# Value's evacuation and its planes in the attention stage: half strips side by side, the last 32 channels moved by DMA

## The chip, the cores and the metric

The kernel runs on one core of a Trainium2 chip. Its time is the device time of one execution in microseconds (us). A core has a tensor engine (PE, with its weight loads listed as PEld), a vector engine (DVE), a scalar engine (ACT), GpSimd (POOL), and the queue engine SP, which issues most of the DMAs. Each engine works through its own instructions in order and waits for others through semaphores. PE writes to PSUM; DVE and ACT read it, POOL does not.

## The reference

Input x is 4 images of 96 channels by 128 x 128 pixels. Layer 0 adds a selective state-space block (scans in four directions over 192 inner channels) to x. Layer 1 adds an attention convolution, and the change lies in that layer:

```python
xr, x1, x2 = _relu_split_norm(x, sc1, sc2, res_coef, nc1, nc2)
# in _attn_conv(x1, x2, aw1, aw2, aw3), every _conv2d being 3x3 over 96 channels:
key = _unfold_nonoverlap(_conv2d(x1, aw1, pad), K).reshape(B, C, kk, -1)
qry = _unfold_nonoverlap(_conv2d(x2, aw2, pad), K).reshape(B, C, kk, -1)
attn = jnp.einsum('bckl,bqkl->bqck', key, qry)
attn = jax.nn.softmax(attn.reshape(B, C, C * kk) / sqrt(C * kk), axis=2)
value = _conv2d(x1, aw3, pad)
y1 = conv2d(value, attn as 3x3 weights)          # per image
y2 = layer_norm(_conv2d(x2, w_conv2, K // 2)) * x1
out = xr + _conv2d(concat(layer_norm(y1), y2), w_full, 0) + b_full
```

So four convolutions are made from the two maps x1 and x2: key and value from x1, query and the second convolution ("c2") from x2. Value is then convolved once more, with weights that depend on all of key and query.

## The kernel before

**Stages.** First come projections and scans of layer 0, then image 0's convolutions by nine taps (direct_maps), and from about 3670 us the attention of the images: image 0's last convolution, and for images 1 to 3 a map stage and a last convolution each. While one image is in attention ("left"), the next image's output projection, its norm and split (ssm_output, split_norm) and the previous image's final output run beside it ("light"). co_run interleaves the two streams by costs that the generators yield; the order in which instructions are written, and a scheduler that puts each engine's instructions in a fixed order before the run, set what every engine does next.

**Convolution by planes.** A row of 128 pixels is cut in TW = 4 runs of TN = 32 with a border element each (pitch PB = 33, row PP = 132). From it planes_of builds NP = 6 sums, the planes, of 32 elements per row: ACT scales the tile into x4 and x2 (scaled, L1404 and L1405), POOL forms ten sums and differences (differences and sums, L1413 to L1418 and L1383), and store_planes writes them to DRAM (L1426 on SP). x4, x2 and pl are single tiles where value is concerned (bufs=1). A later convolution loads planes (ya, yc), and six small products per position replace nine taps. products writes them to three PSUM tiles "two", of which the pool has three buffers; outputs then copies the tiles "ends" and "odd" to SBUF on ACT (L1526) and combines them on DVE into four interleaved outputs (L1540 to L1548, four scalar_tensor_tensor per output part).

**The map stage.** A strip is AR = 12 rows (the eleventh has 8), handled in the order map 0 (x1), map 1 (x2). For each map, "first" products give 128 output channels of the whole strip: 96 of key or query and, in partitions 96 to 128, the last 32 of value or c2. They go to a ring tile of two strips, whose rows are stored by remainder of three (row pitch JW = 135, runs at pitch JB = 34), and PairTaps later transposes and multiplies them into the attention logits sm. The "second" products give the first 64 channels of value or c2 for both half strips at once, in partitions 0 to 64 and 64 to 128. Later is a queue of callbacks: each tick of products runs what is due, `later(f, n)` runs f n ticks after the next one.

**Value and c2 before.** All of value is gathered in own, 128 x 12 rows x 132: the last 32 channels by four POOL copies per strip from the ring to own[96:128] (L1983, after cut has zeroed a border at L1725), the first 64 by the evacuation of the second products to own[0:64], one part per half strip:

```python
to = [(64 * q, 64 * q + 64, vv[0:64, q * hr : (q + 1) * hr]) for q in range(2)]
```

value_out then builds planes of each half strip over all 128 partitions, the second three ticks after the first, and stores them in two DMAs each (vp<-pl). c2's last 32 channels use partitions 64 to 96 of own: four POOL copies (L1983) and one DMA (L1987) per strip; its first 64 go to oc as 128 x 192.

**Constants.** zeros is 133 wide and clears the borders of the DRAM maps with one DMA each (new_map L1262, where L388 to L391); mean192 is 96 wide.

Of the kernel before, what the change touches and what calls it, by code (L numbers as in the profile page):

```python
# [9 lines left out]
F32 = mybir.dt.float32  # L10
# [7 lines left out]
C = 96  # L18
# [53 lines left out]
def kernel(  # L72
# [87 lines left out]
    mean192 = filled(1.0 / (2 * C), "mean192")  # L160
    zeros = filled(0.0, "zeros", PW + 4)
# [6 lines left out]
    signs = const.tile([128, 1], F32, name="signs", tag="signs")  # L168
    nc.vector.memset(signs[64:96], 1.0)
    nc.vector.memset(signs[96:128], -1.0)  # L170
    eps = const.tile([128, 1], F32, name="eps", tag="eps")
    nc.vector.memset(eps, LN_EPS)

# [48 lines left out]
    def other_weights():  # L222
# [9 lines left out]
        with (  # L232
            tc.tile_pool(name="w0", bufs=1, side="right") as w0,
            tc.tile_pool(name="ps0", bufs=1, space=PSUM, side="right") as ps0,
        ):
            wf = w0.tile([RANK, NK, 2 * C], F32, name="wf")
            nc.gpsimd.dma_start(wf, dt_wT)
            outw = w0.tile([C, 2, C], F32, name="outw")
            nc.sync.dma_start(outw, out_wT)
            one = w0.tile([3, 128], BF16, name="one")  # L240
            nc.vector.memset(one, 1.0)
            nc.vector.memset(wdt, 0.0)
            nc.vector.memset(wbc, 0.0)
            yield
            flat = "p k c -> p (k c)"
            pieces = split3(w0, wf.rearrange(flat), [RANK, NK * 2 * C])
            for row, ch, g, p, n in (
                (row, *part)
                for img, *part in PARTS
                for row in ((KI * img,) if part[1] == 1 else (0, 64))  # L250
            ):
                for w in range(3):
                    yield
                    src = pieces[w].rearrange("p (k c) -> p k c", k=NK)[:, :, ch : ch + n]
                    for i in range(3):
# [14 lines left out]
            nc.vector.tensor_add(outbs, pb, outb)  # L270

            pw = ps0.tile([C, C], F32, name="pw")
            for j in range(2):
                nc.tensor.matmul(
                    pw, lhsT=mean192, rhs=outws[:, j], start=(j == 0), stop=(j == 1)
                )
            nc.vector.tensor_sub(outws, outws, pw.unsqueeze(1).to_broadcast([C, 2, C]))
        yield wdt, wbc, outws, outbs
# [75 lines left out]
    def project_weights(pool):  # L354
# [4 lines left out]
        with tc.tile_pool(name="wq", bufs=1, side="left") as pq:  # L359
# [28 lines left out]
            nc.sync.dma_start(where[:, 0:PW], zeros[0:1, 0:PW])  # L388
# [3 lines left out]
            nc.sync.dma_start(where[:, (H + 1) * PW :], zeros[0:1])  # L392
# [869 lines left out]
    def new_map(name):  # L1262

        m = dram.tile([C, (H + 2) * PW + 4], F32, name=name, tag=name, bufs=1)
        nc.sync.dma_start(m[:, 0:PW], zeros[:, 0:PW])
        nc.sync.dma_start(m[:, (H + 1) * PW :], zeros[:, 0 : PW + 4])
        return m

    def new_planes(name):
# [92 lines left out]
                eng.dma_start(w3[p : p + 32, j], wd[64:96, 2, i])  # L1362
        return w1, w2, w3

    def planes_of(later, pool, t, r, then, most=RS, vector=False, bufs=2, p=C):

        a2 = AA * AA
        v = t[:, : r * PP].rearrange("p (h x) -> p h x", x=PP)  # L1370

        def planes(name, bufs):
            pl = pool.tile([p, NP, most * TN], F32, name=name, bufs=bufs)[:, :, : r * TN]
            return pl, [pl[:, i].rearrange("p (h t) -> p h t", t=TN) for i in range(NP)]

        def sums(eng, mid, outer, to):
            f1, f2 = mid[:, :, 0:TN], mid[:, :, PB : PB + TN]
            f3, f0 = outer[:, :, 0:TN], outer[:, :, TN:]
# [20 lines left out]
            later(lambda: then(pl))  # L1399

        def scaled():
            x4 = pool.tile([p, most * PP], F32, name="x4", bufs=bufs)[:, : r * PP]
            x2 = pool.tile([p, most, 2, PB], F32, name="x2", bufs=1)[:, :r]
            nc.scalar.mul(x4, t[:, : r * PP], a2)  # L1404
            nc.scalar.mul(x2, v.rearrange("p h (k b) -> p h k b", b=PB)[:, :, 0:TW:2], AA)  # L1405
            later(lambda: differences(x4.rearrange("p (h x) -> p h x", x=PP), x2))

        def differences(x4, x2):
            mid, outer = x4[:, :, : 2 * PB], x4[:, :, 2 * PB : 2 * PB + 2 * TN]
# [3 lines left out]
            sub(mid, v[:, :, 2 * PB :], mid)  # L1413
            sub(outer, v[:, :, 1 : 1 + 2 * TN], outer)
            sub(to[4], v[:, :, 3 * PB : 3 * PB + TN], v[:, :, PB : PB + TN])
            sub(d1, x2[:, :, 1, 0:TN], d1)
            add(to[3], to[4], d1)
            sub(to[4], to[4], d1)  # L1418
# [278 lines left out]
    class PairTaps(Taps):  # L1697
# [3 lines left out]
        def __init__(self, ps, later, pool):  # L1701
            self.ps, self.later, self.pool = ps, later, pool
            self.taps = [(0, 5), (5, KK)]
            self.sm = pool.tile([C, KK, C], F32, name="sm")
            self.rings = [
                pool.tile([128, 2, AR, JW], F32, name=f"ring{i}", tag=f"ring{i}") for i in range(2)
            ]
# [225 lines left out]
    def attention(img, at):  # L1933
# [4 lines left out]
        def both(*fs):  # L1938
            return lambda: [f() for f in fs if f]

        own = p1.tile([128, AR * PP], F32, name="own")
        if not img.mapped:
            taps = PairTaps(ps, later, pm)
            nc.gpsimd.memset(own, 0.0)
            last = own[64:96, : AR * W]
            vv = own.rearrange("p (h j b) -> p h j b", j=TW, b=PB)[:, :, :, 0:TN]

            def value_out(r0, r):

                def f():  # L1950
                    hr = r // 2
                    for i, a in enumerate((0, hr)):

                        def then(pl, a=a):
                            store_planes(nc.sync, img.vp[0:64], r0 + a, hr, pl[0:64])
                            store_planes(nc.sync, img.vp[64:96], r0 + a, hr, pl[96:128])

                        later(planes_of(
                            later, pm, own[:, a * PP :], hr, then, AR // 2, bufs=1, p=128
                        ), 3 * i)  # L1960

                return f

            for s, (r0, r) in enumerate(chunks):
                hr = r // 2
                for m in (0, 1):
# [2 lines left out]
                    to = taps.rows(m, s, r3)  # L1969

                    def first_out(m=m, s=s, r0=r0, r=r, r3=r3, to=to):
                        if m:
                            for j, v in enumerate(to):
                                nc.vector.bn_stats(
                                    img.c2a[96:128, TW * (r0 // AR) + j], v[96:128, :r]
                                )
                            d = last.rearrange("p (h j t) -> p h j t", j=TW, t=TN)
                        else:
                            taps.cut(s, r3)
                            d = vv[96:128]  # L1980
                        d = d[:, :r3].rearrange("p (i q) j t -> p q i j t", q=3)
                        for j, v in enumerate(to):
                            nc.gpsimd.tensor_copy(  # L1983
                                d[:, :, :, j], v[96:128].rearrange("p (q i) t -> p q i t", q=3)
                            )
                        if m:
                            nc.sync.dma_start(  # L1987
                                img.c2d[64:96, r0 * W : (r0 + r) * W], last[:, : r * W]
                            )

                    evac = outputs(
                        p2, 128, r3 * TN, [(0, 128, to)], later, first_out
# [647 lines left out]
```

## Time and profile before

| what | value |
|---|---|
| median of 3 runs | 6518.25 us (6508.8 to 6521.92) |
| the profiled execution | 6520.08 us, of which its span is 6518.3 us |
| granted clock of PE, mean over the span | 0.886 |
| value's plane builds on ACT, L1404 with L1405 | 66 of each, 863 and 543 ns |
| value and c2 copies on POOL, L1983 | 264, 505 ns |
| value's evacuation of second products, L1548 | 64x192, mean 351 ns (3840 to 4150 us) |
| store of c2's last 32 channels, L1987 | 33 issues on SP, 0.318 us each |

Times are given from the start of the span. In a row of groups, a name such as `own<-ring` is the tile written and the tile read, then come shapes as partitions x elements, the count, the busy time and the mean of one. In a timeline row, the first two numbers are start and duration, and the bracket at its end is the time the engine sat idle before it and what released it. In a source view, "sat idle before it until" lists who released the line's instructions, the idle time in us and how often.

### The profile page before, as it was taken

To read this page: it belongs to the slowest core of one execution; us is meant where nothing else is said; L and a number is where in the kernel's file an instruction comes from. 1 tells how busy PE (TensorE), PEld (TensorE's weight loads), DVE (VectorE), ACT (ScalarE), POOL (GpSimd) and SP (SyncE) were. 2 spreads that over 40 slices of the span, in tenths; PEclk is the share of its full clock that TensorE was granted. 3 is DMA by queue.
4 is the path that set the end of the run, shared out by engine and by line. 5 is a ranking of instruction groups with operands and counts; after the bars stand their busy time and mean duration, and the time that the engine had idled before them with its cause. 6 is when DMAs were issued, how large, how long until landed. Compare 5 with 4: busy or idle time off the path is not lost. (4 is left out here: it accounts for less than half of the span.)

```text
span 6518.3 us, 76253 instructions
## 1 busy us (share of the span) xinstructions
PE 5323.7 (82%) x23264; PEld 2300.7 (35%) x23264; DVE 4813.2 (74%) x7265; ACT 3816.2 (59%) x4800; POOL 3426.6 (53%) x2799
## 2 busy tenths in 40 slices
PE   6889988987887845989988588877878777888888
PEld 2333323322222111444433234444333444344553
DVE  4247778988998768989745885587774787887766
ACT  1247768777787676777624564476544664544642
POOL 2236757978888546969621444456133474033320
PEclk9999989998998666999998788988988888999989
DMA  7766777775766757675666766655776555865658
GB/s 160 175 158 185 199 206 195 217 205 162 219 179 170 218 162 225 197 208 173 200 190 184 195 193 164 171 154 159 198 203 168 151 153 157 223 179 147 185 151 217
DMA packets 865060, 1198.52 MB, mean 184 GB/s; under 512 B 215598, under 2 KB 716054, under 8 KB 852172
## 3 DMA queue, kind: packets, MB, share of 16 engines
q1 hardware_dynamic: 841036, 1138.70, 63.8%
q0 software_dynamic: 16208, 38.42, 2.2%
q10 hardware_dynamic: 7408, 16.53, 0.8%
q8 instruction: 187, 3.06, 0.2%
q14 instruction: 221, 1.81, 0.1%
HBM read 777.82 MB, written 345.62 MB: 172 GB/s over the span
## 5 line engine op out<-in xcount | busy, mean ns | idle before, releaser
L624 PE MATMUL bank<-y,wp 128*128 128x512 f32 (+3 forms) x3584 | 1312.4, 623 | 85.6 <-DMA y<-y 34.9
L857 POOL TENSOR_TENSOR y<-y,dl 128x1024 f32<-128x1024 f32 x384 | 1057.1, 2753 | 267.3 <-DVE dl L849 244.1
L824 POOL TENSOR_TENSOR dl<-dl,u 128x1024 f32<-128x1024 f32 x384 | 1010.4, 2631 | 252.8 <-ACT dA L800 124.1
L845 DVE TENSOR_TENSOR_SCAN dA<-dA,pBC 128x512 f32<-128x512 f32 x768 | 981.6, 1278 | 30.7
L1453 PE MATMUL two<-ya,wd 128*64 128x192 f32 (+3 forms) x2376 | 591.2, 425 | 222.5 <-ACT odd L1526 116.5
L624 PEld LDWEIGHTS bank<-y,wp 128*128 128x128 f32 (+3 forms) x3584 | 457.3, 169 | 753.0 <-issue 651.8
L738 PE MATMUL pBC<-xr,wbc 60*128 60x512 bf16 (+1 forms) x1536 | 462.2, 405 | 315.6 <-DVE dA L845 243.3
L849 DVE TENSOR_TENSOR dl<-dA,pBC 128x512 f32<-128x512 f32 x768 | 528.4, 688 | 258.2 <-PE pBC L738 185.8
L2112 PE MATMUL bank<-y,wn 128*64 128x384 f32 (+5 forms) x2408 | 673.8, 505 | 53.2 <-DMA y<-x1d 28.1
L1912 ACT COPY yb<-ya 64x768 f32<-64x768 f32 (+1 forms) x660 | 537.8, 815 | 207.5 <-PE two L1453 123.0
L667 ACT ACTIVATE dl<-pd,dtb 128x512 f32<-128x512 f32 x768 | 486.2, 684 | 188.7 <-PE pd L738 172.8
L1453 PE MATMUL two<-yb,wd 128*64 128x192 f32 (+3 forms) x2376 | 562.4, 407 | 1.9 <-ACT yb L1912 1.9
L828 DVE TENSOR_TENSOR pBC<-dl,pBC 128x512 f32<-128x512 f32 x768 | 527.6, 687 | 7.3 <-POOL dl L824 6.3
L2112 PEld LDWEIGHTS bank<-y,wn 128*64 128x64 f32 (+3 forms) x2408 | 309.3, 168 | 345.5 <-issue 178.5
L800 ACT ACTIVATE dA<-dl,negA 128x1024 f32<-128x1024 f32 x384 | 420.3, 1141 | 2.3
L1453 PEld LDWEIGHTS two<-ya,wd 128*64 128x64 f32 (+1 forms) x2376 | 265.2, 171 | 433.4 <-ACT odd L1526 126.1
L738 PEld LDWEIGHTS <-wbc 60*128 60x128 bf16 (+1 forms) x1536 | 103.6, 96 | 762.7 <-issue 749.5
L667 ACT ACT_TABLE_LOAD x248 | 318.2, 1283 | 92.1 <-PE pd L738 78.1
L2221 POOL MEMSET o<- 1x1024 f32 x60 | 56.4, 947 | 573.6 <-PE bank L2276 244.5
L1453 PEld LDWEIGHTS two<-yb,wd 128*64 128x64 f32 (+1 forms) x2376 | 293.0, 171 | 146.2 <-issue 34.4
L1004 PE MATMUL bank<-y,outws 96*96 96x512 f32 x512 | 307.7, 737 | 8.2 <-DVE r L1017 6.0
L1383 POOL TENSOR_TENSOR pl<-x 128x192 f32<-128x192 f32 (+2 forms) x456 | 307.8, 690 | 0.2
(317 smaller groups left out, 9532.9 us busy)
## 6 DMA issues: line engine op xcount, KB each, us to landing
u<-zb SPq DMA_DIRECT2D x192, 1024.0 KB
yms<-y SPq DMA_DIRECT2D x96, 512.0 KB
y<-yms SPq DMA_DIRECT2D x64, 768.0 KB
xn<-xnew SPq DMA_DIRECT2D x128, 384.0 KB
ya<-vp SPq DMA_DIRECT2D x120, 336.0 KB
y<-y SPq DMA_DIRECT2D x128, 258.2 KB
zb<-z SPq DMA_DIRECT2D x64, 512.0 KB
ya<-x1p SPq DMA_DIRECT2D x90, 336.0 KB
```

Source lines behind the costliest of these rows:

```text
L624: nc.tensor.matmul(blocks(pz[p:e]), lhsT=ws[k][:, d, c : c + e - p], rhs=window(ys[k], at, d, n), start=(i == 0), stop=(i == len(terms) - 1),)
L667: nc.scalar.activation(dst, src, AF.Softplus, bias=bias)
L738: nc.tensor.matmul(p, lhsT=w[rows], rhs=xr[rows, at : at + CH], start=True, stop=True)
L800: nc.scalar.activation(live[m]["dA"], live[m]["dl"], AF.Exp, scale=negA[:, g % 3, k : k + 1])
L824: nc.gpsimd.tensor_mul(t, t, u_view(n))
L828: nc.vector.tensor_mul(p, live[n]["dl"][:, bass.ts(half, CH)], p)
L845: nc.vector.tensor_tensor_scan(h, h, p, init, ALU.mult, ALU.add)
L849: nc.vector.tensor_mul(live[n]["dl"][:, sl], live[n]["dA"][:, sl], live[n]["C", half])
L857: nc.gpsimd.tensor_add(v, v, t.rearrange("p (a b) -> p a b", b=W))
L1453: nc.tensor.matmul(of(to[p:e], r), lhsT=w[:, i, c : c + e - p], rhs=tiles(t[k][PAIR[i]][:, SLOT[i]], o, r), start=(k == 0), stop=False,)
L1912: nc.scalar.copy(yb[k][64 * h - 64 : 64 * h, :, :n], ya[k][0:64, :, h * TN : h * TN + n])
L2112: nc.tensor.matmul(pc[p:e, :n].rearrange("p (h w) -> p h w", w=W), lhsT=w[:, c : c + e - p], rhs=v[:, :, 0:W], start=(i == 0), stop=(i == ...
```

## The change

Value's first 64 channels are evacuated as one part of 128 partitions: the first half strip in partitions 0 to 64, the second in 64 to 128 of a tile of six rows. One plane build serves both. The last 32 channels are not copied by POOL; DMAs on SP move the ring's rows, with the ring's pitch, into a second tile, few, in which four half strips (those of two strips) stand in partitions 0, 32, 64 and 96. After every second strip, and after the last, one build makes the planes of all of them, three ticks after the other build. planes_of takes the pitch as arguments for this. c2's last 32 channels use partitions 96 to 128 of the tile sm, which were unused: for each third of the ring's rows one POOL copy to one of two slots there, and one DMA from it. The evacuation of the first products, the order of products and all costs that pace co_run stay. To make room, zeros is 72 wide and maps are cleared in two DMAs each, mean192 is 32 wide with a full one made where it is needed, and signs, which nothing reads, is gone.

```diff
+    def clear(to):
+        for a in range(0, to.shape[1], 72):
+            v = to[:, a : min(a + 72, to.shape[1])]
+            nc.sync.dma_start(v, zeros[: v.shape[0], : v.shape[1]])
...
-    def planes_of(later, pool, t, r, then, most=RS, vector=False, bufs=2, p=C):
+    def planes_of(later, pool, t, r, then, most=RS, vector=False, bufs=2, p=C, pb=PB, pp=PP):
...
-            self.sm = pool.tile([C, KK, C], F32, name="sm")
+            sm = pool.tile([128, KK, C], F32, name="sm")
+            self.sm = sm[0:C]
+            self.spare = sm[96:128].rearrange("p t o -> p (t o)")
...
-        own = p1.tile([128, AR * PP], F32, name="own")
+        half = AR // 2
+        own = p1.tile([128, half * (PP + JW)], F32, name="own")
...
-                    for i, a in enumerate((0, hr)):
-                        def then(pl, a=a):
-                            store_planes(nc.sync, img.vp[0:64], r0 + a, hr, pl[0:64])
-                            store_planes(nc.sync, img.vp[64:96], r0 + a, hr, pl[96:128])
-                        later(planes_of(
-                            later, pm, own[:, a * PP :], hr, then, AR // 2, bufs=1, p=128
-                        ), 3 * i)
+                    later(planes_of(
+                        later, pm, first, hr, stores(0, 64, halves), half, bufs=1, p=128
+                    ))
+                    to = [(r0 - r, hr), (r0 - hr, hr)] + halves if s % 2 else halves
+                    if s % 2 or r0 + r == H:
+                        n = 32 * len(to)
+                        later(planes_of(
+                            later, pm, few[:n], hr, stores(64, 96, to), half, bufs=1, p=n,
+                            pb=JB, pp=JW,
+                        ), 3)
...
+            def value_rows(s, r, v):
+                def f():
+                    hr, slots = r // 2, (r + 2) // 3
+                    for i in range(slots):
+                        for h in range(2):
+                            a, e = max(3 * i, h * hr), min(3 * i + 3, (h + 1) * hr)
+                            if a < e:
+                                k = 32 * (2 * (s % 2) + h)
+                                nc.sync.dma_start(
+                                    few[k : k + 32, (a - h * hr) * JW : (e - h * hr) * JW],
+                                    v[:, i + (a - 3 * i) * slots : i + (e - 1 - 3 * i) * slots + 1 : slots],
+                                )
+                return f
+
+            def c2_rows(r0, r, v):
+                slots = (r + 2) // 3
+                for i in range(slots):
+                    n = min(3, r - 3 * i)
+                    t = taps.spare[:, i % 2 * 3 * W : (i % 2 * 3 + 3) * W]
+                    nc.gpsimd.tensor_copy(
+                        t.rearrange("p (q j t) -> p q j t", j=TW, t=TN),
+                        blocks(v[:, i], 3, slots * JW, JB, TW, TN),
+                    )
+                    at = (r0 + 3 * i) * W
+                    nc.sync.dma_start(img.c2d[64:96, at : at + n * W], t[:, : n * W])
...
-                            d = last.rearrange("p (h j t) -> p h j t", j=TW, t=TN)
+                            c2_rows(r0, r, v)
                         else:
                             taps.cut(s, r3)
-                            d = vv[96:128]
-                        for j, v in enumerate(to):
-                            nc.gpsimd.tensor_copy(
-                                d[:, :, :, j], v[96:128].rearrange("p (q i) t -> p q i t", q=3)
-                            )
-                        if m:
-                            nc.sync.dma_start(
-                                img.c2d[64:96, r0 * W : (r0 + r) * W], last[:, : r * W]
-                            )
+                            later(value_rows(s, r, v), 1)
...
-                        to = [
-                            (64 * q, 64 * q + 64, vv[0:64, q * hr : (q + 1) * hr])
-                            for q in range(2)
-                        ]
-                        then = value_out(r0, r)
+                        to = [(0, 128, vv[:, :hr])]
+                        then = value_out(s, r0, r)
```

More of the change, by code (lines that the diff above doesn't have):

```diff
@@ L159 @@
     mean96 = filled(1.0 / C, "mean96")
-    mean192 = filled(1.0 / (2 * C), "mean192")
-    zeros = filled(0.0, "zeros", PW + 4)
+    mean192 = filled(1.0 / (2 * C), "mean192", 32)
+    zeros = filled(0.0, "zeros", 72)
+    def clear(to):
+        for a in range(0, to.shape[1], 72):
+            v = to[:, a : min(a + 72, to.shape[1])]
+            nc.sync.dma_start(v, zeros[: v.shape[0], : v.shape[1]])
     patches = const.tile([128, 1], F32, name="patches", tag="patches")
@@ L166 @@
         nc.sync.dma_start(patches[p : p + 1], zeros[0:1, 0:1])
-    signs = const.tile([128, 1], F32, name="signs", tag="signs")
-    nc.vector.memset(signs[64:96], 1.0)
-    nc.vector.memset(signs[96:128], -1.0)
     eps = const.tile([128, 1], F32, name="eps", tag="eps")
@@ L270, in other_weights @@
             nc.vector.tensor_add(outbs, pb, outb)
+            mean = w0.tile([C, C], F32, name="mean")
+            nc.vector.memset(mean, 1.0 / (2 * C))
             pw = ps0.tile([C, C], F32, name="pw")
@@ L274, in other_weights @@
                 nc.tensor.matmul(
-                    pw, lhsT=mean192, rhs=outws[:, j], start=(j == 0), stop=(j == 1)
+                    pw, lhsT=mean, rhs=outws[:, j], start=(j == 0), stop=(j == 1)
                 )
@@ L387, in project_weights @@
             where = dram.tile([1, (H + 2) * PW + 4], F32, name="where", bufs=1)
-            nc.sync.dma_start(where[:, 0:PW], zeros[0:1, 0:PW])
+            clear(where[:, 0:PW])
             nc.sync.dma_start(
@@ L391, in project_weights @@
             )
-            nc.sync.dma_start(where[:, (H + 1) * PW :], zeros[0:1])
+            clear(where[:, (H + 1) * PW :])
             taps = dram.tile([KK + 1, H * PW], F32, name="taps", bufs=1)
@@ L1264, in new_map @@
         m = dram.tile([C, (H + 2) * PW + 4], F32, name=name, tag=name, bufs=1)
-        nc.sync.dma_start(m[:, 0:PW], zeros[:, 0:PW])
-        nc.sync.dma_start(m[:, (H + 1) * PW :], zeros[:, 0 : PW + 4])
+        clear(m[:, 0:PW])
+        clear(m[:, (H + 1) * PW :])
         return m
@@ L1363, in product_stack, with blocks @@
         return w1, w2, w3
-    def planes_of(later, pool, t, r, then, most=RS, vector=False, bufs=2, p=C):
+    def blocks(t, rows, pitch, step, n, width):
+        return bass.AP(t.tensor, t.offset, [t.ap[0], (pitch, rows), (step, n), (1, width)])
+    def planes_of(later, pool, t, r, then, most=RS, vector=False, bufs=2, p=C, pb=PB, pp=PP):
         a2 = AA * AA
-        v = t[:, : r * PP].rearrange("p (h x) -> p h x", x=PP)
+        v = t[:, : r * pp].rearrange("p (h x) -> p h x", x=pp)
+        over = pb - 1
         def planes(name, bufs):
-            pl = pool.tile([p, NP, most * TN], F32, name=name, bufs=bufs)[:, :, : r * TN]
+            pl = pool.tile([128 if p < C else p, NP, most * TN], F32, name=name, bufs=bufs)[:p, :, : r * TN]
             return pl, [pl[:, i].rearrange("p (h t) -> p h t", t=TN) for i in range(NP)]
         def sums(eng, mid, outer, to):
-            f1, f2 = mid[:, :, 0:TN], mid[:, :, PB : PB + TN]
-            f3, f0 = outer[:, :, 0:TN], outer[:, :, TN:]
+            f1, f2 = mid[:, :, 0:TN], mid[:, :, pb : pb + TN]
+            f3, f0 = outer[:, :, 0:TN], outer[:, :, over:]
             for i, op, x, y in (
@@ L1401, in scaled @@
         def scaled():
[L1402 to L1406, printed above, removed]
+            q = 128 if p < C else p
+            x4 = pool.tile([q, most * JW], F32, name="x4", bufs=bufs)[:p, : r * pp]
+            x2 = pool.tile([q, most, 2, PB], F32, name="x2", bufs=1)[:p, :r]
+            nc.scalar.mul(x4, t[:, : r * pp], a2)
+            nc.scalar.mul(x2, blocks(t, r, pp, 2 * pb, 2, PB), AA)
+            later(lambda: differences(x4.rearrange("p (h x) -> p h x", x=pp), x2))
         def differences(x4, x2):
-            mid, outer = x4[:, :, : 2 * PB], x4[:, :, 2 * PB : 2 * PB + 2 * TN]
+            mid, outer = x4[:, :, : 2 * PB], x4[:, :, 2 * pb : 2 * pb + over + TN]
             d1 = x2[:, :, 0, 0:TN]
@@ L1412, in differences @@
             sub, add = nc.gpsimd.tensor_sub, nc.gpsimd.tensor_add
-            sub(mid, v[:, :, 2 * PB :], mid)
-            sub(outer, v[:, :, 1 : 1 + 2 * TN], outer)
-            sub(to[4], v[:, :, 3 * PB : 3 * PB + TN], v[:, :, PB : PB + TN])
+            sub(mid, v[:, :, 2 * pb : 2 * pb + 2 * PB], mid)
+            sub(outer, v[:, :, 1 : 1 + over + TN], outer)
+            sub(to[4], v[:, :, 3 * pb : 3 * pb + TN], v[:, :, pb : pb + TN])
             sub(d1, x2[:, :, 1, 0:TN], d1)
@@ L1939, in both, with value_out, stores, then @@
             return lambda: [f() for f in fs if f]
-        own = p1.tile([128, AR * PP], F32, name="own")
+        half = AR // 2
+        own = p1.tile([128, half * (PP + JW)], F32, name="own")
         if not img.mapped:
             taps = PairTaps(ps, later, pm)
[L1944 to L1948, printed above, removed]
-                def f():
-                    hr = r // 2
-                    for i, a in enumerate((0, hr)):
-                        def then(pl, a=a):
-                            store_planes(nc.sync, img.vp[0:64], r0 + a, hr, pl[0:64])
-                            store_planes(nc.sync, img.vp[64:96], r0 + a, hr, pl[96:128])
+            first, few = own[:, : half * PP], own[:, half * PP :]
+            nc.gpsimd.memset(first, 0.0)
+            vv = first.rearrange("p (h j b) -> p h j b", j=TW, b=PB)[:, :, :, 0:TN]
+            def value_out(s, r0, r):
+                hr = r // 2
+                halves = [(r0, hr), (r0 + hr, hr)]
+                def stores(c0, c1, to):
+                    def then(pl):
+                        for i, (at, n) in enumerate(to):
+                            store_planes(
+                                nc.sync, img.vp[c0:c1], at, n,
+                                pl[(c1 - c0) * i : (c1 - c0) * (i + 1), :, : n * TN],
+                            )
+                    return then
+                def f():
+                    later(planes_of(
[4 more added lines that the diff above has]
+                        n = 32 * len(to)
@@ new lines, in c2_rows @@
+            def c2_rows(r0, r, v):
[6 more added lines that the diff above has]
+                        blocks(v[:, i], 3, slots * JW, JB, TW, TN),
+                    )
+                    at = (r0 + 3 * i) * W
+                    nc.sync.dma_start(img.c2d[64:96, at : at + n * W], t[:, : n * W])
@@ L1971, in first_out @@
                     def first_out(m=m, s=s, r0=r0, r=r, r3=r3, to=to):
+                        v = taps.rings[m][96:128, s % 2]
                         if m:
-                            for j, v in enumerate(to):
+                            for j, x in enumerate(to):
                                 nc.vector.bn_stats(
-                                    img.c2a[96:128, TW * (r0 // AR) + j], v[96:128, :r]
+                                    img.c2a[96:128, TW * (r0 // AR) + j], x[96:128, :r]
                                 )
-                            d = last.rearrange("p (h j t) -> p h j t", j=TW, t=TN)
+                            c2_rows(r0, r, v)
                         else:
                             taps.cut(s, r3)
-                            d = vv[96:128]
-                        d = d[:, :r3].rearrange("p (i q) j t -> p q i j t", q=3)
-                        for j, v in enumerate(to):
-                            nc.gpsimd.tensor_copy(
-                                d[:, :, :, j], v[96:128].rearrange("p (q i) t -> p q i t", q=3)
-                            )
-                        if m:
-                            nc.sync.dma_start(
-                                img.c2d[64:96, r0 * W : (r0 + r) * W], last[:, : r * W]
-                            )
+                            later(value_rows(s, r, v), 1)
                     evac = outputs(
```

## The prediction

> **What bounds the kernel now.** I read the page first, then windows over the stages that the change touches, then the timelines of PE and ACT inside one strip, then the source views of the lines concerned. The busy row of the page:
>
> ```profile
> PE 5323.7 (82%) x23264; PEld 2300.7 (35%) x23264; DVE 4813.2 (74%) x7265; ACT 3816.2 (59%) x4800; POOL 3426.6 (53%) x2799
> ```
>
> PE leads, so time is to be won where PE idles. The edited code runs in the map stages of images 1 to 3, about 3820 to 4527, 4735 to 5500 and 5700 to 6290 us. The windows view (busy time of PE, PEld, DVE, ACT, POOL, then granted clock) cuts the first two images into their output-projection and split phases; the last row is image 3:
>
> ```profile
> 3846.00:4240.00 394.00, 333.49 (x1957) 166.56 (x1956) 231.28 (x464) 192.60 (x257) 194.07 (x282) 0.90 0.61 165
> 4240.00:4527.00 287.00, 211.31 (x1461) 136.57 (x1460) 233.97 (x466) 194.01 (x286) 180.14 (x267) 0.84 0.57 152
> 4770.00:5105.00 335.00, 285.58 (x1393) 123.91 (x1391) 187.49 (x356) 146.21 (x190) 130.92 (x182) 0.89 0.64 174
> 5105.00:5460.00 355.00, 270.41 (x1925) 172.14 (x1926) 295.50 (x560) 240.29 (x349) 235.07 (x348) 0.87 0.56 153
> 5721.00:6286.00 565.00, 490.50 (x3123) 286.68 (x3124) 418.91 (x680) 285.95 (x358) 224.05 (x347) 0.92 0.60 165
> ```
>
> PE is busy 74 to 87% there and no other engine is full. Adding up the idle times in PE's timeline gives 141, 175 and 86 us for the three images, of which 95, 92 and 44 us (231 together) end with an ACT copy out of PSUM (ends, odd, kt). Why ACT is late shows in strip 6 of image 2 (ACT, then PE, then three windows of 4 us):
>
> ```profile
> 5248.32 0.86 ACT L1404 ACTIVATE x<-own 128x792 f32<-128x792 f32 x1 [3.90 <-POOL pl L1383]
> 5249.09 2.35 ACT L1245 ACTIVATE bank<-xn,kept 96x512 f32<-96x512 f32 x3
> 5252.36 0.78 ACT L1526 COPY odd<-two 128x768 f32<-128x768 f32 x1
> ...
> 5253.19 0.91 PE L1453 MATMUL two<-ya,wd 128*64 128x192 f32 x4 [6.65 <-ACT odd L1526]
> ...
> 5247.00:5251.00 4.00, 0.00 (x0) 0.00 (x0) 1.11 (x2) 2.57 (x4) 3.58 (x7) 0.67 0.61 144
> 5251.00:5255.00 4.00, 1.81 (x12) 1.40 (x14) 3.86 (x6) 2.30 (x4) 4.00 (x6) 0.50 0.13 43
> 5255.00:5259.00 4.00, 3.92 (x32) 2.22 (x30) 4.00 (x8) 3.98 (x7) 4.00 (x5) 0.55 0.24 56
> ```
>
> Value's planes are built twice per strip, once per half, in the single tiles x4 and x2. The second half's scaling on ACT waits until POOL has finished with the first half's. ACT's later copy "odd" stands behind it, and PE behind that; then PE runs at half clock until about 5258.3. The source views of the two scalings:
>
> ```profile
>   POOL pl L1418: 96.6, 43
> ...
>   POOL pl L1383: 95.8, 32
> ```
>
> Of the 96.6 us at L1405, 47.7 belong to value (own), the rest to split_norm's x1 (half); the 95.8 us at L1404 all belong to value. So value's second builds cost ACT 143 us of idling.
>
> **The Trainium skill.** "TensorE: Matmul & The Clock Gate", Part 1, says that an idle window of about 3.4 us halves the clock and a busy one restores it. The trace agrees: 1.00 before the gap above, 0.50 after it. "DMA: Bandwidth & Descriptors", the section on the anatomy of one DMA, says that a semaphore wait of a DMA is served on the sequencer that issues it, and puts about 2 us of fixed cost on a transfer, most of it the receipt of the write. The trace has more: POOL's 4 KB transfer at L990 lands in 3.6 us (below).
>
> **Part by part.**
>
> 1. Plane builds. Before, 2 per strip, 22 per image. After, one per strip for the 64 channels of both halves (128 partitions) and one for the last 32 at strips 1, 3, 5, 7, 9 and 10: 17. So 15 fewer in three images; strips 0, 2, 4, 6, 8 lose their second build. A build is 0.863 + 0.543 = 1.41 us of ACT (L1404, L1405) and on POOL 0.884 + 0.866 + 0.532 + 0.608 + 0.593 + 0.592 + 4 x 0.591 = 6.44 us: 21 us of ACT and 97 us of POOL gone. What reaches PE: for each of the 15 strips I took the second build's POOL wait plus its durations on ACT, and the PE wait for ACT that follows within 6 us of it, and counted the smaller: image 1 5.6, 0, 0, 2.5, 6.1; image 2 4.1, 1.7, 2.5, 6.7, 4.7; image 3 2.3, 1.3, 5.3, 0, 2.4; sum 45 us. Eight of these waits are 4 us or longer in all and are followed by half clock; the one shown loses half of 5253.2 to 5258.3, 2.5 us, so 8 x 2.5 = 20 us more. Ceiling 65 us. When this wait is gone, the next is late: the PSUM pair that DVE frees, or the copy kt. I take two thirds, 43 us. Odd strips keep two builds three ticks apart and are counted at nothing.
>
> 2. The value copies. For map 0, four POOL copies per strip (L1983) go: 33 x 4 x 0.505 = 67 us of POOL. POOL's wait for the ring there does not go: cut (L1725) still waits for it. In their place value_rows issues 4 DMAs per strip on SP, which wait for the same DVE writes, one tick later. What is queued behind them on SP is loads of ya two strips ahead, xn and y of the next image. They are wanted by a build at least half a strip later, so I cost their landing at nothing; if the cover were gone, each strip would pay about 4 us.
>
> 3. DVE. Value's evacuation of the second products falls from 8 instructions of 64x192 (351 ns) to 4 of 128x192 (344 ns, as at oc): 264 x 0.351 - 132 x 0.344 = 47 us of DVE, 1.4 us a strip. PE's waits that end with DVE's ring, own or sm are 73 of its 402 us of idling in the three stages; I count an eighth, 6 us.
>
> 4. SP. 132 DMAs for value_rows and 4 instead of 1 for c2 (3 at the last strip, so 129 for 33): 228 more at 0.31 us (L1987: 0.318) are 71 us of SP over some 2000 us, beside SP's waits of 10 us and more; nothing. At the start clear issues 6 more DMAs at 0.64 us (vp<-zeros): 3.8 us; I count 2. The smaller memset at L1944 and the constants are nothing.
>
> 5. The new wait. c2_rows has two slots: the third copy of a strip needs the store of the first to have landed, the fourth that of the second. The trace shows no such store's landing; the nearest row is at L990:
>
> ```profile
> DMA to landing us min/median/max: 1.5/3.6/7.9
> ```
>
> From the end of the first copy: 0.3 us of SP, the landing, less the second copy's 0.5 us: 1.3 to 7.7 us a strip, 3.4 taken. Behind the third copy on POOL stand split_norm's x1 differences and the adds of r (L1025), for which ACT and DVE wait. Image 3 has only memsets there. So 22 strips x 3.4 = 75 us of POOL; POOL is busy 54% in the first four windows above, so 40 us collide, and about a third gets through to PE: 13 us lost. Ends: 1.3 us gives 5; 7.7 us with half getting through gives 46. Below nothing is excluded: no wait becomes shorter by it.
>
> Sum: -43 - 6 + 2 + 13 = -34 us. The profiled execution took 6520.1 us (span 6518.3 and 1.8 around it), the median of the runs is 6518.25; 6520 - 34 = 6486 on the one, 6484 on the other, which I forecast.
>
> **Rivals.**
>
> The gain reaches the odd strips too. POOL loses 164 us of work and ACT 21 us, and in the split phase of image 2 POOL stands at 66%; second builds in odd strips (10 us of PE wait at strip 5) shorten as well. Against: x4 and x2 stay single. The full ceiling of 65, DVE at 16 and 10 for the odd strips, less 15: 6442.
>
> Nothing measurable. PE's next releaser is just as late, because DVE is busy 83% in the split phases (233.97 of 287, 295.50 of 355). For: where ACT waited 2 to 6 us in image 1's strips 2 to 5, PE had no wait. Then a third of 65, 22, against 15: 6511.
>
> Slower, by the new wait at the third c2 copy. If SP is held when the first store's turn comes (SP's waits for PE at L1895 are 4 to 14 us each), POOL stands 15 us and more per strip. With a third of the colliding time reaching PE, a strip's 12 us eat the 49 us gained (22 x 12 x 0.54 / 3 = 48); with two thirds, 6 us do. At 12 us and two thirds: 6518 - 49 + 95 + 2 = 6566; at 16 us and a third 6535, which I take for this case. Against: POOL in image 3 has 60% idle and the wait costs nothing there.
>
> That the spare partitions tie the copies to DVE's writes of sm is a rival by name only: own already held POOL's c2 rows in partitions of their own beside DVE's writes, and the source view names no wait of DVE for that store.
>
> **How the numbers follow.** Forecast 0.53, the larger gain 0.17, nothing measurable 0.13, slower 0.17. A measurement tells 0.2%, 13 us, from no change. The first two are faster: 0.70. For 8 in 10 the range runs from just below the larger gain, 6435, to just above the slower case, 6540; the likeliest case's own is 6460 to 6505.
>
> **What would show it.** Right: own-builds 51 with L1404's wait for POOL near half of 95.8 us; PE's idling behind ACT in the three stages down from 231 to about 185 us; own evacuations of 128x192, 132 of them; the granted clock up by about 0.01 in the map stages; waits of POOL for the c2 store near 110 us. Wrong: PE's idling the same under another releaser (DVE wide or ring), or POOL's waits for that store over 250 us with ACT and DVE waiting for POOL in the first two images.

## The result, and the profile after

| | before | changed |
|---|---|---|
| median of 6 runs each, us | 6516.3 (6508.8 to 6521.9) | 6462.5 (6441.3 to 6482.8) |
| ratio to before | | 0.9916 (0.9895 to 0.9936) |
| the profiled execution, and its span | 6520.08, 6518.3 | 6482.78, 6481.0 |

The changed kernel is 54 us faster; the interval allows 42 to 68. The forecast was 34. The profiled execution is the slowest of the six, 37 us below the one of before, so the sums over its trace fall short of the medians by about 17 us. A second profile of the changed kernel (e0_after below) has a span of 6448.4; where the two differ, both are given.

Two rows of the page of the changed kernel, the busy row and the group of the products that wait for ACT (line numbers have moved from before to after, near these lines by 10 to 13: L1464 was L1453, and L1537 was L1526):

```profile
PE 5325.5 (82%) x23264; PEld 2306.2 (36%) x23264; DVE 4757.0 (73%) x7132; ACT 3792.2 (59%) x4770; POOL 3279.9 (51%) x2514
...
L1464 PE MATMUL two<-ya,wd 128*64 128x192 f32 (+3 forms) x2376 | 588.8, 422 | 197.8 <-ACT odd L1537 80.0
```

PE's work is unchanged. POOL has lost 147 us and 285 instructions, DVE 56 us and 133 instructions. Before, the same group had 222.5 us of idling, of which 116.5 ended with "odd". The windows view, one row for each whole map stage of images 1, 2 and 3 (busy time of PE, PEld, DVE, ACT, POOL, then clock, DMA share, GB/s), of the kernel before:

```profile
3820.80:4539.10 718.30, 568.12 (x3535) 315.35 (x3534) 498.86 (x995) 403.09 (x565) 390.30 (x572) 0.87 0.60 161
4668.40:5501.80 833.40, 654.29 (x3678) 341.87 (x3677) 603.36 (x1101) 437.26 (x593) 398.90 (x578) 0.86 0.61 165
5688.50:6304.50 616.00, 525.49 (x3313) 305.56 (x3314) 459.65 (x750) 311.16 (x388) 225.12 (x349) 0.91 0.60 165
```

and of the changed kernel:

```profile
3830.70:4550.10 719.40, 581.18 (x3535) 319.57 (x3533) 474.08 (x937) 391.36 (x550) 328.46 (x467) 0.86 0.61 160
4674.50:5495.90 821.40, 656.86 (x3678) 347.16 (x3676) 568.18 (x1042) 430.08 (x582) 338.25 (x472) 0.86 0.63 169
5678.30:6264.90 586.60, 512.88 (x3314) 300.34 (x3314) 445.03 (x706) 302.15 (x378) 184.96 (x254) 0.94 0.66 177
```

The stages take +1, -12 and -29 us (in the second profile -1, -10 and -34). POOL loses 62, 61 and 40 us in them, 163 together, as the forecast counted (164). In image 3, of 29 us, 17 are idling of PE and 12.6 PE's busy time, which shrinks as the clock rises from 0.91 to 0.94. In image 1 PE idles 11 us less, but the same 3535 products take 13 us longer at a lower clock, and nothing is left. Added up over the three stages, PE's waits ended by ACT fall from 248 to 203 us (200 in the second profile); those ended by DVE stay at 144 (137).

The strip that the forecast showed, strip 6 of image 2 counted from 0, in the timeline of the changed kernel (start, duration):

```profile
5249.18 0.91 PE L1464 MATMUL two<-ya,wd 128*128 128x384 f32 x2 [1.99 <-ACT kt L1762]
...
5250.45 0.53 ACT L1416 ACTIVATE x<-own 128x396 f32<-128x396 f32 x1
5250.89 0.85 ACT L1415 ACTIVATE x<-own 128x792 f32<-128x792 f32 x1
...
5252.80 0.91 PE L1464 MATMUL two<-ya,wd 128*128 128x384 f32 x2
...
5254.91 0.78 ACT L1537 COPY ends<-two 128x768 f32<-128x768 f32 x1
```

and the same three windows of 4 us:

```profile
5247.00:5251.00 4.00, 2.01 (x9) 1.19 (x8) 3.17 (x8) 3.98 (x7) 2.17 (x2) 1.00 0.99 262
5251.00:5255.00 4.00, 4.00 (x15) 1.98 (x14) 3.31 (x3) 2.17 (x4) 3.99 (x7) 1.00 0.89 207
5255.00:5259.00 4.00, 4.00 (x19) 1.87 (x17) 4.00 (x5) 2.38 (x4) 4.00 (x6) 1.00 1.07 283
```

The strip's only build runs without a wait for POOL. PE waits 1.99 us for the copy kt, and then goes on at full clock, where before it idled 6.65 us and then ran at half clock. The forecast's windows of that strip begin inside the gap of 6.65 us; these rows of the kernel before show its beginning:

```profile
5246.00:5247.00 1.00, 0.54 (x7) 0.37 (x5) 0.97 (x2) 0.00 (x0) 1.00 (x2) 1.00 0.92 282
5247.00:5248.00 1.00, 0.00 (x0) 0.00 (x0) 0.00 (x0) 0.00 (x0) 1.00 (x3) 1.00 0.99 236
5248.00:5249.00 1.00, 0.00 (x0) 0.00 (x0) 0.00 (x0) 0.68 (x1) 0.84 (x2) 0.68 0.21 61
```

PE's last product ends near 5246.5, and the clock falls near 5248.4, 1.8 us into the gap. So the two levels of the clock are as the forecast says, but the 3.4 us of idling that it quotes are not what this strip shows; and the gap of 1.99 us in the changed kernel left the clock at 1.00. The source views of the two scalings (this line is from L1415, formerly L1404):

```profile
  POOL pl L1393: 25.8, 9
```

and this one from L1416, formerly L1405:

```profile
  POOL pl L1429: 44.4, 14
```

Before, they were 95.8 and 96.6. Value's builds alone wait 40 us for planes, formerly 143; the rest belongs to split_norm's builds.

### The profile page after: what moved, and what is told of

It reads as the page before. It is cut to its first block, busy times and chain, and to the rows that moved or that the text cites. A ratio compares the mean times of both kernels' runs of the same rounds, so it can differ in the third digit from the quotient of the medians.

```text
span 6481.0 us, 76143 instructions
## 1 busy us (share of the span) xinstructions
PE 5325.5 (82%) x23264; PEld 2306.2 (36%) x23264; DVE 4757.0 (73%) x7132; ACT 3792.2 (59%) x4770; POOL 3279.9 (51%) x2514
## 5 line engine op out<-in xcount | busy, mean ns | idle before, releaser
L1464 PE MATMUL two<-ya,wd 128*64 128x192 f32 (+3 forms) x2376 | 588.8, 422 | 197.8 <-ACT odd L1537 80.0
L1464 PE MATMUL two<-yb,wd 128*64 128x192 f32 (+3 forms) x2376 | 563.5, 407 | 4.0 <-ACT yb L1925 4.0
L1464 PEld LDWEIGHTS two<-ya,wd 128*64 128x64 f32 (+1 forms) x2376 | 265.9, 169 | 398.5 <-ACT odd L1537 90.6
L1464 PEld LDWEIGHTS two<-yb,wd 128*64 128x64 f32 (+1 forms) x2376 | 293.7, 171 | 147.3 <-issue 34.1
L1464 PE MATMUL two<-ya,wa 128*96 128x384 f32 (+1 forms) x528 | 231.1, 521 | 71.8 <-DMA wa<-watd 27.0
```

Of the source, the lines that this page charges most:

```text
L1464: nc.tensor.matmul(of(to[p:e], r), lhsT=w[:, i, c : c + e - p], rhs=tiles(t[k][PAIR[i]][:, SLOT[i]], o, r), start=(k == 0), stop=False,)
```

## The experiments

Each kernel ran beside the kernel before on one chip. Its median there was 6505 us, 6503, 6505 and 6518 for the groups e0 to e3, e4 to e8, e9 to e13 and e14. So the ratios are what is to be compared. "After" is the changed kernel. Stage lengths come from the profiles, one each; the whole times and ratios from 4 to 27 runs. "ACT's waits for planes" are ACT's idle times in the three map stages that end with POOL's work on planes, for value's builds and split_norm's together: 182 us before and 68 in e0_after. Value's builds alone have 143 and 39 of them.

**e0_after: the changed kernel, unedited.**

> The changed kernel as it is, beside its variants on one chip. Both theories expect about 0.992 of the kernel before (6462 of 6516 us), and a profile in which the stages before 3650 us end as in the kernel before: the 10 us by which they ended later in the first profile of the changed kernel would then be scatter.

0.9907 (0.9891 to 0.9922), 6443 us: the gain repeats, 62 us here. Stages 718, 823 and 582 us.

**e1_each_strip: after, but the last 32 channels get a build in every strip.**

```diff
-                    to = [(r0 - r, hr), (r0 - hr, hr)] + halves if s % 2 else halves
-                    if s % 2 or r0 + r == H:
+                    to = halves
+                    if True:
...
-                                k = 32 * (2 * (s % 2) + h)
+                                k = 32 * h
```

> The changed kernel, but the last 32 channels get a plane build in every strip (64 partitions, two half strips) instead of one for two strips: 22 builds per image again. Theory 1 (the gain comes from the second builds that are gone, and ACT's wait for POOL with them): most of the gain goes, 6490 to 6510 us, ACT's waits of own builds for POOL back above 100 us. Theory 2 (the gain comes from DVE's and POOL's lighter copies and evacuations): it stays, 6460 to 6475 us.

0.9976 (0.9964 to 0.9988), 6486 us: 43 us of the gain are gone. The windows view of this kernel, the three map stages:

```profile
3802.00:4533.20 731.20, 580.78 (x3536) 322.37 (x3534) 482.49 (x937) 397.76 (x560) 356.84 (x517) 0.85 0.59 157
4658.80:5487.40 828.60, 658.58 (x3677) 344.75 (x3676) 575.01 (x1041) 436.77 (x592) 370.88 (x526) 0.87 0.62 167
5670.20:6266.30 596.10, 519.15 (x3314) 303.74 (x3314) 449.22 (x706) 308.38 (x388) 224.96 (x304) 0.92 0.64 173
```

POOL has 98 us more than in e0_after, ACT 20, and the stages take 14, 6 and 14 us more. But ACT's waits for planes rise only from 68 to 81 us, those of value's builds hardly at all (39 to 41), and PE's waits for ACT do not rise (195). So the extra builds cost what the forecast put on the builds, but not by its route, ACT held behind a build. Their route was not found. PE's waits for DVE rise from 137 to 170 us, but e9 below, which is as fast as the change, has 166. DVE's waits for POOL rise from 94 to 111, and DVE is busy 17 us longer with as many instructions; neither was followed to PE.

**e8_skip_even: before, with the second build left out at even strips** (but not the last). Both halves then store the first half's planes, so the second half's planes of value are left out there.

```diff
-                    for i, a in enumerate((0, hr)):
+                    once = r0 // AR % 2 == 0 and r0 + r < H
+                    for i, a in enumerate((0,) if once else (0, hr)):
...
```

> The kernel before, but in strips 0, 2, 4, 6 and 8 of a map stage only the first half's planes are built, and stored for both halves: the second half's planes are left out, so the rows stored there are the first half's. 15 builds fewer, with the same number of stores, the same evacuation and copies. Theory 1: this alone gives most of the change's gain, 6470 to 6485 us beside 6516. Rival (evacuation and copies made the gain): 6500 to 6520 us.

0.9951 (0.9939 to 0.9964), 6473 us: 31 us, with the 15 builds as the only thing removed. PE's waits for ACT fall from 248 to 214, ACT's waits for planes from 182 to 120. Value's builds wait 86 us instead of 143; the 57 us that went are what the second builds of these 15 strips waited before (58). The map stages are 23, 2 and 10 us shorter than before:

```profile
3810.10:4505.70 695.60, 559.59 (x3536) 312.61 (x3534) 492.25 (x989) 396.39 (x555) 355.12 (x521) 0.88 0.60 165
4624.10:5455.70 831.60, 679.96 (x3678) 355.31 (x3678) 599.03 (x1101) 431.67 (x583) 368.97 (x528) 0.84 0.60 166
5640.20:6245.90 605.70, 523.85 (x3313) 304.74 (x3314) 460.38 (x750) 304.70 (x378) 196.63 (x299) 0.91 0.60 168
```

**e3_pool_rows: after, value's rows moved by POOL copies again instead of DMAs.**

```diff
-                                nc.sync.dma_start(
-                                    few[k : k + 32, (a - h * hr) * JW : (e - h * hr) * JW],
+                                nc.gpsimd.tensor_copy(
+                                    few[k : k + 32, (a - h * hr) * JW : (e - h * hr) * JW].rearrange("p (a b) -> p a b", b=JW),
```

> The changed kernel, but the ring's rows go to the four-half-strip tile by four POOL copies a strip instead of four DMAs. Theory 1: the 67 us of POOL are hidden, within 10 us of the changed kernel. Rival (POOL's load is what counts, because ACT waits for POOL): 20 to 40 us slower than the changed kernel.

0.994 (0.9926 to 0.9954), 6469 us: 26 us of the gain are gone (by the two intervals some 8 to 35), for 74 us more of POOL busy time in the stages. ACT's waits for planes rise from 68 to 128 us, those of value's builds from 39 to 79, and DVE's waits for POOL from 94 to 138. The 67 us of copies that were expected to be hidden were not.

**e2_two_parts: after, the evacuation of 128 x 192 as two parts of 64 x 192.**

```diff
-                        to = [(0, 128, vv[:, :hr])]
+                        to = [
+                            (64 * q, 64 * q + 64, vv[64 * q : 64 * q + 64, :hr])
+                            for q in range(2)
+                        ]
```

> The changed kernel, but value's second products leave PSUM as two parts of 64x192 again, to the two halves of the same tile: 8 instructions on DVE instead of 4. Theory 1: 6 us slower than the changed kernel, 6460 to 6475 us. Rival (DVE's 47 us are on the path): 6490 to 6510 us.

0.9924 (0.9913 to 0.9936), 6459 us: 16 us above e0_after, with intervals that overlap, so that a cost is not shown. DVE's busy time in the stages is 51 us higher.

**e4_one_slot and e9_four_slots: after, with one slot for c2's rows, or four.** In e9 the third and fourth slot lie in those partitions of few that the other strip's rows use.

```diff
-                    t = taps.spare[:, i % 2 * 3 * W : (i % 2 * 3 + 3) * W]
+                    t = taps.spare[:, 0 : 3 * W]
```

```diff
-                    t = taps.spare[:, i % 2 * 3 * W : (i % 2 * 3 + 3) * W]
+                    k = 0 if s % 2 else 64
+                    t = (taps.spare if i < 2 else few[k : k + 32])[:, i % 2 * 3 * W : (i % 2 * 3 + 3) * W]
```

> The changed kernel, but c2's last 32 channels use one slot in the spare partitions instead of two: three waits of a copy for a store in each strip, where there were two of which one stands. If POOL's new wait is priced as forecast (13 us for about 3.4 us a strip), this adds about 20 to 40 us; if the scheduler fills the wait with other work, less than 10 us.

> The changed kernel, but c2's last 32 channels have four slots: two in the spare partitions, two in the partitions of the four-half-strip tile that are free at that time. No copy waits for a store of its own strip. If the wait costs what was forecast, 13 us faster than the changed kernel, 6425 to 6440 us where that stands at 6443; from the 40 us that a single slot cost, up to 25 us. If the scheduler hides the two-slot wait: no change.

e4: 0.9969 (0.9957 to 0.9981), 6486 us, 36 above e6 (6450), which ran beside it and is as fast as the change. e9: 0.9916 (0.9899 to 0.9933), the same as the change. The waits of the c2 copies, in the source view of L2012 in the changed kernel:

```profile
L2012 POOL COPY sm<-ring x129: 501/506/1582, 3883.1 to 6241.8; 32x384 f32<-32x384 f32 x129
...
  DVE ring L1559: 80.7, 19
  issue: 79.2, 12
  DMA c2d<-sm: 30.4, 9
```

and in e4_one_slot:

```profile
  DMA c2d<-sm: 79.2, 35
```

With two slots POOL waits for a store 9 times in the 33 strips, with one slot 35 times, and that kernel is slower. With two, the order mostly has other POOL work between the second copy and the third (the third starts 12 us after the first in the median), so that the store has landed. One of the nine, in the timeline of the changed kernel:

```profile
5153.17 0.96 POOL L2012 COPY sm<-ring 32x384 f32<-32x384 f32 x2 [12.49 <-issue]
5153.70 0.77 SPq L2017 DMA_DIRECT2D c2d<-sm  x2
5155.35 0.98 POOL L2012 COPY sm<-ring 32x384 f32<-32x384 f32 x2 [1.22 <-DMA c2d<-sm]
```

The first store is issued at 5153.70, and the third copy starts 1.65 us later, near the shortest landing that the forecast took (1.5).

**e12_before_pool_scale: before, the second build's two scalings on POOL instead of ACT.** So ACT is never held by a second build; in exchange POOL has the scalings to do.

```diff
-            nc.scalar.mul(x4, t[:, : r * PP], a2)
-            nc.scalar.mul(x2, v.rearrange("p h (k b) -> p h k b", b=PB)[:, :, 0:TW:2], AA)
+            x2s = v.rearrange("p h (k b) -> p h k b", b=PB)[:, :, 0:TW:2]
+            if pool_scale:
+                nc.gpsimd.tensor_scalar(x4, t[:, : r * PP], a2, None, ALU.mult)
+                nc.gpsimd.tensor_scalar(x2, x2s, AA, None, ALU.mult)
+            else:
+                nc.scalar.mul(x4, t[:, : r * PP], a2)
+                nc.scalar.mul(x2, x2s, AA)
...
+                            pool_scale=(i == 1),
```

> The kernel before, but the second half's two scalings run on POOL instead of ACT. No work goes: POOL gains about 1.4 us a build (45 us in all), ACT loses 1.41 us a build and, above all, need not wait for POOL there. Theory 1 (ACT held by the second build delays PE): faster by 15 to 40 us, 6465 to 6490 us of 6505, PE's wait for the copy odd down from 159 to about 110 us. Rival (POOL's amount of work is what counts): equal or slower, 6505 to 6530 us.

0.9992 (0.9983 to 1.0001), 6499 us: hardly anything in all, where the forecast's mechanism was to give 15 to 40 us. By stages two things seem to cancel. Its map stages in the windows view:

```profile
3812.00:4548.40 736.40, 583.49 (x3536) 323.53 (x3534) 499.98 (x992) 390.06 (x543) 422.40 (x592) 0.84 0.58 156
4673.10:5521.10 848.00, 675.98 (x3678) 353.24 (x3678) 607.86 (x1101) 424.14 (x571) 433.75 (x600) 0.83 0.59 162
5708.70:6296.70 588.00, 511.53 (x3314) 299.33 (x3314) 464.05 (x750) 296.97 (x366) 276.03 (x371) 0.94 0.62 173
```

In image 3, POOL rises to 276 of 588 us busy, and the stage is 28 us shorter than before (588 against 616), nearly what the whole change gives it (587), with the same clock of 0.94. In images 1 and 2, where POOL also works for split_norm and the next image's sums, the stages are 18 and 15 us longer. The scalings are dear on POOL; their first source view, of L1406:

```profile
L1406 POOL TENSOR_SCALAR x<-own x33: 1530/2190/3043, 3864.9 to 6265.9; 128x792 f32<-128x792 f32 x30, 128x528 f32<-128x528 f32 x3
```

The other, of 128 x 396, takes 1.21 us: 3.4 us per build, 112 us in all, where 45 were expected. PE's waits for ACT are 37 us in image 3, formerly 45, but 96 and 107 in images 1 and 2, formerly 97 and 105. So ACT held behind the second builds seems to cost time in image 3; that in images 1 and 2 POOL's amount of work outweighs it is a likely reading, not a shown one. These are single profiles. Image 3's stage took 574 to 587 us in the five profiles of kernels as fast as the change (its own two, e6, e9 and e14), so 28 us are more than that scatter. The 15 and 18 us may be no more than another order of instructions: e3's image 1 is 16 us shorter than that of e0_after, though POOL has more to do there.

**e13_few_pool_scale: after, the scalings of the last 32 channels' build on POOL** (the same edit, with `pool_scale=True` on few's build).

> The changed kernel, with the scalings of the build of the last 32 channels on POOL instead of ACT (18 builds). Theory 1: what is left of ACT's waits for POOL in own builds (68 us) shrinks to a third, 5 to 15 us faster than the changed kernel. Rival: equal or up to 10 us slower, POOL having 25 us more to do.

0.993 (0.9914 to 0.9946), 6459 us: 10 us above e9, which ran beside it and is as fast as the change; the intervals overlap. POOL has some 63 us more, and ACT's waits for planes fall further, from 68 to 41 us, those of value's builds to nothing. No gain shows; but since POOL has more to do, this does not tell what that wait alone is worth.

**e14_c2_on_dve: e9 with the c2 copies on DVE.**

```diff
-                    nc.gpsimd.tensor_copy(
+                    nc.vector.tensor_copy(
```

> The changed kernel with four slots for c2's last 32 channels, and the copies into them on DVE instead of POOL (129 of 32x384). POOL loses 65 us of work. If POOL's load sets the pace in images 1 and 2 (26 us for 67 us of POOL, by the run with POOL copies of the ring's rows), 10 to 25 us faster than the changed kernel, less what some 40 us more of DVE cost; 6425 to 6440 us where the changed kernel stands at 6443. Rival (DVE's load counts as much): 6440 to 6460 us.

0.9911 (0.9895 to 0.9927), as the change. POOL has 68 us less in the stages than in e9, DVE 45 more; neither better nor worse.

**e5_before_later and e6_few_later: ticks.** Before, the second build six ticks after the first instead of three; after, few's build six ticks after the other.

```diff
-                        ), 3 * i)
+                        ), 6 * i)
```

```diff
-                        ), 3)
+                        ), 6)
```

> The kernel before, with the second half's build six ticks after the first instead of three. No work goes, only ACT's wait for POOL should. Theory 1: the own builds' waits for POOL fall from 148 us to below 60, and the time by 15 to 35 us, to 6480 to 6500 us. Rival (the work counts, not the wait): no change, 6505 to 6525 us.

> The changed kernel, with the build of the last 32 channels six ticks after the other instead of three. Theory 1: the rest of the own builds' waits for POOL (41 us) goes too, 5 to 20 us faster than the changed kernel. Rival: no change.

e5: 1.0001 (0.9992 to 1.001). e6: 0.9916 (0.9903 to 0.9929), as the change. The source view of L1404 in e5:

```profile
  POOL pl L1383: 96.0, 31
```

The wait that e5 was to take away is as long as before (95.8), and the other scaling's is 76.8. In the median the second build follows the first by 3.5 us on ACT, as before, and in e6 few's build follows the other by 11.4 us, as in the changed kernel. So the ticks hardly moved the builds, and neither run decides anything about the waits.

## Why the prediction was right, and where its sizes were off

**Direction and bound.** Faster, in the likeliest case's direction, and 6462 lies within that case's own range (6460 to 6505), at its edge. Of the signs that it named, these came: 132 evacuations of 128 x 192, own-builds 51, PE's waits for ACT 45 us lower (46 forecast). These came out otherwise: L1404's wait for POOL fell to about a quarter of 95.8 us, not to half; the granted clock rose in image 3 alone; POOL's waits for the c2 store are 30 us, not 110. The gain came out 20 to 28 us larger than the forecast; the two steps that failed, 2 and 5, both err towards too small a gain.

**Step 1, plane builds (-43).** The direction is shown and the size is near: taking the 15 builds alone out of the kernel before gives 31 (e8), putting 15 back into the changed kernel costs 43 (e1). That e1 gives the forecast's very number is luck: two thirds of the ceiling were a guess, and e1's cost does not come by the forecast's route. The chain from POOL over ACT to PE is seen in the strip above and in the waits of e8, and image 3 of e12 fits it; that it is the whole cause is not shown, since e12 takes ACT's wait away and is no faster in all. The strip sum had 14, 20 and 11 us for images 1, 2 and 3; the stages became shorter by nothing, 10 to 12 and 29 to 34, and in e8 by 23, 2 and 10, so a gain by image cannot be read from single profiles. Half clock after a stall was counted as 20 us for all images; in the change the mean clock rose in image 3 alone (0.91 to 0.94), and in e8 it stayed at 0.91 there. "Odd strips at nothing" was too low for the waits: the second builds of the 15 strips had 58 of the 143 us, and 104 went. What the other 46 are worth in time was not measured.

**Step 2, the value copies (0).** This step failed. It gave the 67 us of POOL no worth and no reason for that; e3 shows that they cost 26. POOL works in order, and ACT and DVE wait for what stands behind: both engines' waits for POOL rose. Over e1, e3, e8 and e13, 63 to 98 us of POOL work moved the time by 10 to 43 us, a sixth to under a half; but all of these except e3 also move about 20 us of ACT's work, and e13's 10 are not clear of nothing. Moving 68 us from POOL to DVE (e14) gained nothing. About SP the step was right as far as the trace shows: 10 us of idling in all end with one of the DMAs from the ring, and PE's waits for DMAs in the three stages are 10 us, formerly 4.

**Step 3, DVE (-6).** DVE's saving of 47 us is right (51 in e2); its worth is 16 us by e2's medians, an amount not clear of the 6, nor of nothing.

**Step 4, SP (+2).** A DMA from the ring holds SP 0.613 us, not the 0.31 taken from the c2 store: 132 x 0.3 = 40 us more on SP. No experiment shows a cost. Two more microseconds at the start cannot be told from the scatter: the stages ahead end 10 us later than before in one profile and 13 earlier in the other; over all profiles they end at 3805 to 3821 us in the variants of the kernel before and at 3802 to 3831 in those of the changed one.

**Step 5, c2's new wait (+13).** This step failed too: e9, without the wait, is no faster. The step priced the copies as if back to back, with 3.4 us in each strip; POOL waited 30 us in all, 9 times, and mostly had other work in between. The mechanism is real, since one slot costs 36 us (e4).

**The sum.** The runs give 31 to 43 for the builds, 26 for the copies, 16 for the evacuation, 0 for SP and for c2: 73 to 85, where the change is worth 54 to 62. Each of these has an interval of some 8 us or more to either side, so the excess may be noise; it may also be that the parts overlap, which no run tested. The result lies midway between the forecast and the rival of the larger gain (6442). Of that rival's reasons the full ceiling of step 1 was not found, but the shorter waits in odd strips were, and its 16 us for DVE are e2's medians. The slower case is excluded with two slots; even with one slot the kernel is faster than before (e4, 0.9969).

**What stays open.** Why image 1 gains nothing in the changed kernel: PE's idling falls, its busy time rises by as much, and over all these kernels that stage took 696 to 736 us, with no clear relation to POOL's work (702 in e3, which has more of it than e0_after with 718). Every edit gives the scheduler another order, and differences of some 15 us in one stage can come from that. By which route e1 loses its time was not settled either.

## What to carry to other kernels

In this kernel an engine busy for half the time, which works in order and feeds other engines, had no free work: 67 us of its copies cost 26. So price its instructions by what stands behind them, or undo them alone and measure. A wait of an in-order engine for a fresh store cost little where the order had other work to put in between, so look at the order before pricing it back to back. Copies moved off such an engine by DMAs, on a queue that had slack, were worth something here, while the same engine's copies moved to DVE were not: where the work goes matters as much. An edit that takes a wait away but adds work (e12), or one that the scheduler hardly follows (e5, e6), does not settle which of the two counts.

## What the runs showed of the hardware

- POOL's scaling of 128 x 792 took 2.19 us and of 128 x 396 1.21 us (e12), against 0.863 and 0.543 on ACT: more than twice as long.
- SP took about twice as long to issue a DMA of the ring's rows as one of the plain c2 store before (0.318 us); the source view of L1999 in the changed kernel:

```profile
L1999 SPq DMA_DIRECT2D own<-ring x132: 585/613/1985, 3864.0 to 6225.0; - x132
```

- The same 3535 products of image 1's map stage had PE busy for 560 to 586 us, at mean clocks of 0.88 to 0.84, depending on the kernel around them (e3, e8 and e4; one product more in e3 and e8).
